# Gates and values of two chunks as seven products of halves, and a reordered start, in a pre-norm linear-attention block

## The chip, the cores and the metric

The kernel runs on one core of a Trainium2 chip. The metric is the device time of one execution in microseconds (us). Engines are named as in the profile: PE is TensorE (matrix products), PEld its weight loads, DVE is VectorE, ACT is ScalarE, POOL is GpSimd, SP is SyncE, which here issues nearly all DMAs. Each engine works through its own list of instructions in order; semaphores make one engine wait for another.

## What is computed

Input x is 4 sequences x 2048 tokens x 512 features, float32. Cut to what matters:

```python
xn  = layernorm(x)                                  # no gain
h   = layernorm(xn) * ln_g + ln_b                   # second normalisation, with gain
q, k, v = split(h @ W_qkv + b_qkv, 3)
gate = sigmoid(xn @ W_gate + b_gate); gate /= mean(gate) + EPS
q, k = relu(q * gate)**2 + EPS, relu(k * gate)**2 + EPS      # 16 heads of 32
# causal linear attention: running sums over time of k v^T and of k
out = (q . sum(k v^T)) / (q . sum(k) + EPS)
x = x + out @ W_proj + b_proj
y = layernorm(x)
x = x + gelu(y @ U1 @ V1 + b1) @ U2 @ V2 + b2       # rank 128, 2048 hidden
```

All products are float32. The profile counts one float32 product of a 128x128 block with 128x512 as two PE instructions.

## The kernel before, in words

The 8192 tokens are cut into 64 chunks of 128; a sequence has 16. Chunks are worked in pairs (c, c+1), c even. The order of the work is written out by hand (`tc.manual_schedule()`, line 748): the order of the calls is the order of the instructions on each engine.

- **Normalise.** `moments` (L213) takes mean and variance of a chunk on DVE. `first_norm_factors` (L321) makes scale and shift for four chunks at a time, for chunks from 4 on as a chain of small POOL instructions with Newton steps (`inverse_deviation_by_steps`, L227); `normalize_chunk` (L345) applies them on ACT. `turned` (L304) brings the chunk to features-first form through DRAM with SP's DMAs (`xlT`, four buffers).
- **Gates.** `gate_of` (L367): four products of a 128x128 block of `xlT` with 128x512 of the weights `wg` (L359), one DVE operation out of PSUM (L370), a sigmoid on ACT (L375), a factor on DVE (L379).
- **Queries and keys.** `combinations` (L383) forms four sums and differences of halves of the pair's `xlT` on POOL. `queries_and_keys` (L394) needs both results for both chunks, which is a 2x2 block product in halves (two chunks by two halves of the features; two halves by two outputs). It is done with seven half products instead of eight (the scheme of Strassen and Winograd); one half product is two matrix products. The weights lie in `w7` as seven slots (B11, B21, B22, T4, T1, T2, T3), the differences T1 to T4 are made once at the start (L786 to L789). `square` (L410) applies relu, gate and square, `turn_queries` (L468) and `turn_keys` (L473) turn the results in 32x32 blocks on DVE and through DRAM by DMA (L292 writes, L297 reads).
- **Values.** `values_of` (L460): four products with `wv` per chunk (L359), one DVE add (L463).
- **Attention of a chunk.** `new_keys` (L479) copies the last running sum into column 0 of `kT` on POOL; `keys_of` (L487) fills the rest on ACT; `sums_of` (L496) is a running sum on DVE (L500) and a product with the queries on POOL (L510); `scores_of` (L517) are 16 small products in four PSUM banks, masked by DVE (L534); `inverse_denominators` (L543) is a chain on DVE; `weighted` (L557) makes the numerator, multiplies by the inverse (L587) and adds k v to the state in PSUM (L596). `project_out` (L611) is the output projection, with the residual add (L617) and moments on DVE.
- **Feed-forward of a pair**, one pair behind: `feed_forward` (L649) is a list of small steps (`down`, 16 `hidden` L669 with gelu L671, 16 `gather` L675, two `up` L691). `pump(n)` (L704) emits the next n of them, and so fills PE's list between the steps of attention. `second_norm` (L623) prepares its input with Newton steps on POOL.
- **PSUM.** `bank` (L104) hands out six banks in turn; a product into a bank waits until the result that it held six requests ago was read.
- **The main loop** (L837) runs over pairs: combinations, gates, `down`, queries and keys, then scores and the rest of attention of the last chunk of the pair before (e = c - 1), then the first chunk of this pair, with the values' products between. `first_moments(n)` (L802) calls `first_norm_factors` at each fourth chunk.

Of the kernel before, what the change touches and what calls it, by code (L numbers as in the profile page):

```python
# [51 lines left out]
P = 128  # L53
# [4 lines left out]
def tile_linear_attention_block(  # L58
# [39 lines left out]
    xp = ctx.enter_context(tc.tile_pool(name="xp", bufs=13))  # L98
# [52 lines left out]
    wg, pieces = weights(w_gate, "wg")  # L151
    load(pieces)
    for c in range(1, NJ):
        load_x(c)
    wv, pieces = weights(w_qkv[:, 2 * D : 3 * D], "wv")
    load(pieces)
# [4 lines left out]
    w7 = const.tile([P, 7, NH, D], F32, tag="w7", name="w7")  # L161

    def load_half(slot, half, col):
        for k in range(NH):
            at = (half * NH + k) * P
            nc.sync.dma_start(w7[:, slot, k, :], w_qkv[at : at + P, col : col + D])

    load_half(B11, 0, 0)
    load_half(B21, 1, 0)
    bqkv_one = [row(b_qkv[bass.ts(n, D)], "a", 4, f"bqkv_one_{n}", nc.sync) for n in range(3)]  # L170
    load_half(B12, 0, D)
    load_half(B22, 1, D)
    load_x(NJ)
    wp, pieces = weights(w_proj, "wp")
    load(pieces)
    load_x(NJ + 1)
    load_x(NJ + 2)
# [10 lines left out]
    rows_of = [  # L188
        [w7[:, slot, k, :] for slot in (B11, B21) for k in range(NH)],
        [w7[:, slot, k, :] for slot in (B12, B22) for k in range(NH)],  # L190
        [wv[:, k, :] for k in range(NK)],
    ]
# [111 lines left out]
    def turned(src, to, name):  # L304
        st = blocks(src, name)
        dr = dram.tile([DH, NQ, NK, NQ, DH], F32, tag="drn", bufs=2, name=f"drn_{name}")
        for i in range(NQ):
            nc.sync.dma_start(
                dr[:, :, :, i, :].rearrange("m j k t -> m (j k) t"),
                st[i * DH : (i + 1) * DH].rearrange("m j k t -> m (j k) t"),  # L310
            )
        transfers_back()
        back.append(
            lambda: nc.sync.dma_start(
                to.rearrange("p k t -> p (k t)"), dr.rearrange("m j k i t -> j m (k i t)")
            )
        )
# [3 lines left out]
    def first_norm_factors(chunks, mv):  # L321
# [4 lines left out]
        if chunks[0] < NJ:  # L326
            inverse, engine = inverse_deviation, nc.vector
# [17 lines left out]
    def normalize_chunk(c):  # L345
        norm, n, _ = first_norm[c]
        xl = normalized(x_of[c], norm, n, f"xl_{c}")
        t = work.tile([P, NK, P], F32, tag="xlT", bufs=NJ, name=f"xlT_{c}")
        xlT_of[c] = t
        if c >= NJ:  # L350
            turned(xl, t, f"xl_{c}")

        return lambda: nc.scalar.copy(t, features_first(xl, f"ps_xl_{c}"))  # L353


    def project(c, w, name):
        ps = bank(name)
        for k in range(NK):
            nc.tensor.matmul(  # L359
                ps, xlT_of[c][:, k, :], w[:, k, :], start=(k == 0), stop=(k == NK - 1)  # L360
# [6 lines left out]
    def gate_of(c):  # L367
        ps = project(c, wg, f"ps_g_{c}")
        gate = work.tile([P, D], F32, tag="gate", bufs=2, name=f"gate_{c}")
        nc.vector.scalar_tensor_tensor(gate, ps, first_norm[c][2], bg_row, ALU.mult, ALU.add)  # L370
        return gate

# [21 lines left out]
    def queries_and_keys(c, s, gates):  # L394
# [4 lines left out]
        def half(ps, stationary, slot, more=False):  # L399
            for k in range(NH):  # L400
                nc.tensor.matmul(  # L401
                    ps,
                    stationary[:, k, :],
                    w7[:, slot, k, :],
                    start=(k == 0 and not more),
                    stop=(k == NH - 1),
                    skip_group_check=True,
                )

        def square(c, n, t):  # L410
            gate, rg = gates[c]
            nc.vector.scalar_tensor_tensor(t, t, 0.0, gate, ALU.max, ALU.mult)  # L412
            sq = work.tile([P, D], F32, tag="qk"[n], bufs=(2, 3)[n], name=f"{'qk'[n]}_{c}")
            nc.scalar.activation(sq, t, AF.Square, scale=rg)  # L414
            if n == 0:
                nc.scalar.activation(sq, sq, AF.Identity, bias=eps_col)
# [35 lines left out]
        def second():  # L452
            qT1 = turn_queries(c + 1, q1)
            kq1 = turn_keys(c + 1, k1)
            transfers_back()
            return {c: (k0, qT0, kq0), c + 1: (k1, qT1, kq1)}

        return second

    def values_of(c):  # L460
        ps = project(c, wv, f"ps_v_{c}")
        v = work.tile([P, D], F32, tag="v", bufs=2, name=f"v_{c}")
        return v, lambda: nc.vector.tensor_add(v, ps, bqkv_row[:, 2 * D : 3 * D])  # L463
# [79 lines left out]
    def inverse_denominators(c, qs):  # L543

        back = work.tile([P, H, DH], F32, tag="back", name=f"back_{c}")
        nc.vector.transpose(back.rearrange("p n d -> p (n d)"), qs.rearrange("p g t -> p (g t)"))
        den = work.tile([P, H], F32, tag="den", bufs=2, name=f"den_{c}")
        nc.vector.reduce_sum(den, back, axis=AX.X)
        nc.vector.tensor_scalar_add(den, den, EPS)
        nc.vector.reciprocal(den, den)  # L550
        inv = work.tile([P, NK, P], F32, tag="inv", name=f"inv_{c}")
# [97 lines left out]
    def feed_forward(b):  # L649
# [29 lines left out]
        def both(f):  # L679
# [4 lines left out]
            if f == NF + 1:  # L684
                held["qs"] = work.tile([P, BT], F32, tag="qs", name=f"qs_{b}")
# [29 lines left out]
    def spread(to, one, name):  # L715
        ps = bank(name)
        nc.tensor.matmul(ps, ones[0:1, :], one, start=True, stop=True)
        nc.scalar.copy(to, ps)
# [13 lines left out]
    def gain_in_weights(n):  # L732
        for k in range(NK):
            w = rows_of[n][k]
            nc.scalar.activation(w, w, AF.Copy, scale=g_col[:, k : k + 1])
# [15 lines left out]
    def gate_with_factor(c):  # L751
        gate = gate_of(c)
        total, rg = sigmoid_of(c, gate)
        return lambda: gate_factor(total, rg), (gate, rg)

    mv = new_moments("mv_0")
    gates, values = {}, {}
    moments(x_of[0], mv, 0)
    first_norm_factors([0], mv)
    spread(bg_row, bg_one, "ps_bg")  # L760
    spread(bp_row, bp_one, "ps_bp")
    normalize_chunk(0)()
    for c in range(1, NJ):
        moments(x_of[c], mv, c)
    first_norm_factors(range(1, NJ), mv)
    turn_xl = normalize_chunk(1)
    offset_terms(2)
    g0 = gate_of(0)
    turn_xl()
    gain_in_weights(2)  # L770
    offset_terms(0)
    g1 = gate_of(1)
    offset_sum(2)
    for c, g in ((0, g0), (1, g1)):
        total, rg = sigmoid_of(c, g)
        gate_factor(total, rg)
        gates[c] = g, rg
    gain_in_weights(0)
    offset_terms(1)
    gain_in_weights(1)  # L780
    for c in range(2):
        values[c] = values_of(c)
    turn_xl = [normalize_chunk(c) for c in (2, 3)]
    for c in range(2):
        values[c][1]()
    nc.vector.tensor_sub(w7[:, T1], w7[:, B12], w7[:, B11])  # L786
    nc.vector.tensor_sub(w7[:, T2], w7[:, B22], w7[:, T1])
    nc.gpsimd.tensor_sub(w7[:, T3], w7[:, B22], w7[:, B12])
    nc.gpsimd.tensor_sub(w7[:, T4], w7[:, B21], w7[:, T2])  # L789
    for turn in turn_xl:  # L790
        turn()
    offset_sum(0)
    offset_sum(1)
    spread(b2_row, b2_one, "ps_b2")


    mv_first = mv_second = None
    waiting = []
    pairs = {}
    keys = {}  # L800

# [10 lines left out]
    def sums_and_products(c, kT):  # L812
# [5 lines left out]

    def rest_of_attention(e, scores, inv):
        nonlocal mv_second  # L820
        oT = weighted(e, scores, pairs[e][1], pairs[e][0], values.pop(e)[0], inv)
        return oT
# [7 lines left out]
    finish = []  # L830

    def gates_in_step(c):
        for n in (c, c + 1):
            done, gates[n] = gate_with_factor(n)
            finish.append(done)

    for c in range(0, NC + 1, 2):  # L837
        e = c - 1
        live = c < NC

        if live:
            s_ = combinations(c)
            if c > 2:
                gates_in_step(c)
        if e > 0:
            nc.gpsimd.tensor_add(x_of[e], x_of[e], bp_row)
            inv = inverse_denominators(e, keys[e][1])

        if c >= 4:
            rest += feed_forward((c - 4) // NP)  # L850
            pump(1)
        if live:
            while finish:
                finish.pop(0)()
            if c > 0:
                first_moments(c + NJ + 2)
            second = queries_and_keys(c, s_, gates)
            gates.clear()
        else:
            waiting.pop(0)()  # L860
            transfers_back()
            pump(3)
        if e > 0:
            scores = scores_in_step(e)
        if live:
            pairs.update(second())
        pump(1)
        if live and c > 0:
            values[c] = values_of(c)
        pump(1)  # L870
        if e > 0:
            oT = rest_of_attention(e, scores, inv)
        if live and c > 0:
            values[c][1]()
        pump(1)
        if e > 0:
            project_in_step(e, oT)
            if live:
                kT = new_keys(c)
                waiting += second_norm([e - 1, e], mv_second)  # L880
# [10 lines left out]
        if c == 0:  # L891
            kT = new_keys(c)
            for n in range(NJ, NJ + 3):
                first_moments(n)
        if c + 7 < NC:
            load_x(c + 7)


        c, e = c + 1, c
        if c + 2 < NC:  # L900
            for n in (c + 1, c + 2):
                if n >= NJ:
                    normalize_chunk(n)
        sums_and_products(e, kT)
        nc.gpsimd.tensor_add(x_of[e], x_of[e], bp_row)
        kT = new_keys(c)
        if c == 1:
            gates_in_step(c + 1)
        pump(4)
        scores = scores_in_step(e)  # L910
        inv = inverse_denominators(e, keys[e][1])
        pump(3)
# [3 lines left out]
        if c > 1:  # L916
# [62 lines left out]
```

## Time and profile before

| | |
|---|---|
| runs (us) | 1914.93, 1919.36, 1915.3; median 1915.3 |
| profiled execution (us) | 1920.7 |
| its span (us) | 1918.9 |
| PE busy | 1867.0 us (97%) |
| DVE busy | 1197.8 us (62%) |
| POOL busy | 765.0 us (40%) |
| ACT busy | 646.1 us (34%) |
| mean granted PE clock | 0.988 |
| chain that ended last | PE 94%; DMA 2%; POOL, DVE, ACT, issue 1% each |
| gates (L359) of the pairs start at (us) | 130.16 (4, 5), 194.07 (6, 7), then every 56 to 58 us |

The span is the time from the first to the last instruction; the execution lasts 1.8 us longer. Busy time of PE is not PE at its peak, since the ends of its instructions overlap: 128x512 shows 0.59 us for one, but in a row one starts each 0.43 us. In the lines of a timeline the columns are start (us), duration (us), engine, line, operation, out<-in and count; brackets give the idle time ahead and what ended it.

### The profile page before, as it was taken

To read this page: it belongs to the slowest core of one execution; us is meant where nothing else is said; L and a number is where in the kernel's file an instruction comes from. 1 tells how busy PE (TensorE), PEld (TensorE's weight loads), DVE (VectorE), ACT (ScalarE), POOL (GpSimd) and SP (SyncE) were. 2 spreads that over 40 slices of the span, in tenths; PEclk is the share of its full clock that TensorE was granted. 3 is DMA by queue.
4 is the path that set the end of the run, shared out by engine and by line. 5 is a ranking of instruction groups with operands and counts; after the bars stand their busy time and mean duration, and the time that the engine had idled before them with its cause. 6 is when DMAs were issued, how large, how long until landed. Compare 5 with 4: busy or idle time off the path is not lost.

```text
span 1918.9 us, 34094 instructions
## 1 busy us (share of the span) xinstructions
PE 1867.0 (97%) x12832; PEld 1113.2 (58%) x12832; DVE 1197.8 (62%) x2107; ACT 646.1 (34%) x1112; POOL 765.0 (40%) x1578
## 2 busy tenths in 40 slices
PE   7679999999999999999999999999999999999988
PEld 3336555666555666555666655566655566655556
DVE  5566766566766666666666666666666666666651
ACT  4123333233333233333233333233333233333233
POOL 2433525353443533425353443534435343443330
PEclk9799999999999999999999999999999999999999
DMA  6133323333323333323333323333323333322220
GB/s 203 55 99 88 84 88 87 96 111 89 85 89 90 90 111 91 88 83 91 90 111 92 95 82 87 92 106 92 94 80 94 88 105 101 89 75 80 77 75 31
DMA packets 290577, 175.27 MB, mean 91 GB/s; under 512 B 138726, under 2 KB 239078, under 8 KB 290284
## 3 DMA queue, kind: packets, MB, share of 16 engines
q1 hardware_dynamic: 289350, 173.08, 30.7%
q8 instruction: 101, 1.65, 0.4%
q14 instruction: 64, 0.52, 0.1%
q10 hardware_dynamic: 1062, 0.01, 0.0%
HBM read 90.46 MB, written 82.58 MB: 90 GB/s over the span
## 4 chain that ended last, share of the span: by engine, by line
PE 94%; DMA 2%; POOL 1%; DVE 1%; ACT 1%; issue 1%; SPq 0%; ACTq 0%; DVEq 0%; POOLq 0%
PE ps_h L669 13%; PE ps_Q L675 12%; PE ps_q L401 11%; PE ps_p L614 11%; PE ps_v L359 11%; PE ps_g L359 11%; PE ps_a L524 4%; PE ps_n L578 3%; PE ps_n L567 3%; PE ps_u L401 3%; PE ps_t L401 3%; PE ps_P L656 3%; PE ps_k L401 3%; PE ps_u L691 3%; PE ps_S L596 1%
## 5 line engine op out<-in xcount | busy, mean ns | idle before, releaser
L671 ACT ACTIVATE h<-ps_h,b_col 128x256 f32<-128x256 f32 x512 | 242.5, 474 | 479.9 <-PE ps_h L669 479.6
L669 PE MATMUL ps_h<-pT,v_sb 128*128 128x256 f32 x1024 | 318.2, 393 | 9.2 <-DVE pT L664 9.2
L675 PE MATMUL ps_Q<-h,u_sb 128*128 128x256 f32 x1024 | 295.9, 381 | 1.0 <-ACT h L671 1.0
L614 PE MATMUL ps_p<-wp,oT 128*128 128x512 f32 x512 | 234.5, 601 | 6.3 <-DVE oT L587 6.3
L669 PEld LDWEIGHTS ps_h<-pT,v_sb 128*128 128x128 f32 x1024 | 185.0, 190 | 79.5 <-issue 37.1
L359 PE MATMUL ps_v<-wv,xlT 128*128 128x512 f32 x512 | 230.2, 592 | 0.0
L359 PE MATMUL ps_g<-wg,xlT 128*128 128x512 f32 x512 | 228.4, 599 | 1.4 <-ACT xlT L353 1.4
L675 PEld LDWEIGHTS ps_Q<-h,u_sb 128*128 128x128 f32 x1024 | 192.0, 190 | 31.9 <-ACT h L671 7.0
L401 PE MATMUL ps_q<-w,xlT 128*128 128x512 f32 x384 | 175.9, 594 | 0.0
L476 POOL TENSOR_SCALAR k<-k 128x512 f32<-128x512 f32 x64 | 95.8, 1498 | 199.8 <-DVE blocks_k L276 198.4
L534 DVE TENSOR_TENSOR a<-ps_a,causal 128x512 f32<-128x512 f32 x256 | 158.5, 680 | 25.1 <-PE ps_a L524 25.1
L617 DVE TENSOR_TENSOR x<-ps_p,x 128x512 f32<-128x512 f32 x64 | 44.3, 692 | 206.2 <-PE ps_p L614 163.1
L510 POOL TENSOR_TENSOR qsum<-qT,sums 128x512 f32<-128x512 f32 x64 | 75.3, 1176 | 241.7 <-DVE sums L500 234.0
L359 PEld LDWEIGHTS ps_g<-wg,xlT 128*128 128x128 f32 x512 | 98.2, 192 | 125.1 <-issue 118.5
L614 PEld LDWEIGHTS ps_p<-wp,oT 128*128 128x128 f32 x512 | 98.1, 193 | 104.6 <-issue 94.3
L375 ACT ACTIVATE gate<-gate 128x512 f32<-128x512 f32 x64 | 40.3, 629 | 335.7 <-DVE gate L370 335.7
L359 PEld LDWEIGHTS ps_v<-wv,xlT 128*128 128x128 f32 x512 | 97.1, 190 | 96.1 <-issue 92.6
L414 ACT ACTIVATE k<-u,rg 128x512 f32<-128x512 f32 x64 | 45.7, 714 | 308.6 <-DVE u L412 308.6
L233 POOL TENSOR_SCALAR newton_v<-mv 128x2 f32<-128x2 f32 (+2 forms) x48 | 11.7, 244 | 301.9 <-DVE mv L216 301.9
L401 PEld LDWEIGHTS ps_q<-w,xlT 128*128 128x128 f32 x384 | 73.3, 191 | 79.7 <-issue 69.9
L432 POOL TENSOR_TENSOR u<-u,t 128x512 f32<-128x512 f32 x32 | 40.5, 1265 | 197.0 <-DVE t L430 197.0
L370 DVE SCALAR_TENSOR_TENSOR gate<-ps_g,unscale,bg_row 128x512 f32<-128x512 f32 x64 | 47.9, 750 | 113.6 <-PE ps_g L359 113.6
(143 smaller groups left out, 2886.9 us busy)
## 6 DMA issues: line engine op xcount, KB each, us to landing
x<-in_L_attn_x_dram SPq DMA_DIRECT2D x64, 256.0 KB
dr_k<-blocks_k SPq DMA_DIRECT2D x64, 256.0 KB
dr_q<-blocks_q SPq DMA_DIRECT2D x64, 256.0 KB
kq<-dr_k SPq DMA_DIRECT2D x256, 64.0 KB
qT<-dr_q SPq DMA_DIRECT2D x256, 64.0 KB
out_dram<-x SPq DMA_DIRECT2D x64, 256.0 KB
dr_x<-blocks_x SPq DMA_DIRECT2D x63, 256.0 KB
x2T<-dr_x SPq DMA_DIRECT2D x252, 64.0 KB
```

The source lines that it names most:

```text
L359: nc.tensor.matmul(ps, xlT_of[c][:, k, :], w[:, k, :], start=(k == 0), stop=(k == NK - 1))
L401: nc.tensor.matmul(ps, stationary[:, k, :], w7[:, slot, k, :], start=(k == 0 and not more), stop=(k == NH - 1), skip_group_check=True,)
L476: nc.gpsimd.tensor_scalar_add(k, k, EPS)
L510: nc.gpsimd.tensor_mul(qs.rearrange("p k (i t) -> p k i t", t=DH), qT.rearrange("p i k t -> p k i t"), sums[:, :, 1 : P + 1].rearrange("p ...
L524: nc.tensor.matmul(ps[r][:, bass.ts(g, P)], kT[rows, g, 1 : P + 1], qT[rows, :, g, :], start=True, stop=True,)
L534: nc.vector.tensor_tensor(a, ps[r].rearrange("p (g t) -> p g t", t=P), causal.unsqueeze(1).to_broadcast([P, NK, P]), ALU.mult,)
L567: nc.tensor.matmul(num[rows, bass.ts(g, P)], S[rows, g, :], qT[rows, :, g, :], start=(g == 0), stop=False, skip_group_check=True,)
L578: nc.tensor.matmul(num[r * DH : (r + 1) * DH, bass.ts(g, P)], v[:, h * DH : (h + 1) * DH], scores[r][:, g, :], start=first and g == 0, sto ...
L614: nc.tensor.matmul(ps, oT[:, g, :], wp[:, g, :], start=(g == 0), stop=(g == NK - 1))
L669: nc.tensor.matmul(ps, v1_sb[:, 0, bass.ts(f, P)], held["p"], start=True, stop=True)
L671: nc.scalar.activation(h, ps, AF.Gelu_apprx_tanh, bias=b1_col[:, f : f + 1])
L675: nc.tensor.matmul(held["q"], u2_sb[:, f, :], held["h"].pop(f), start=(f == 0), stop=(f == NF - 1))
```

## The change

Three parts, made together:

1. **Gates and values of a pair** (c >= 4) become one 2x2 block product of halves, with seven half products instead of eight: `gates_and_values`. It uses the pair's `combinations`, which queries and keys have already, and a second set of seven weight slots, `wgv` (gate weights in B11 and B21, value weights in B12 and B22); `w7` is now `wqk`, and `wg` and `wv` are gone. To make room, `xlT` has two buffers instead of four, x tiles 12 instead of 13, the queries are squared in place, and some tiles share buffers.
2. **The start** is written out anew for the first two pairs: gates and values of these are still plain products; pair (2, 3) gets its projections before the attention of chunks 0 and 1. Factors of chunks 4 to 7 are made on ACT and DVE.
3. **The loop** runs for pairs from 4 on, in a new order: inverse denominators of e, x loads, gates and values, scores of e, queries and keys, `down`, the rest of attention of e, and so on. `new_keys` moves into `sums_and_products`; the first moments of two chunks stand together, ahead of it.

```diff
-    xp = ctx.enter_context(tc.tile_pool(name="xp", bufs=13))
+    xp = ctx.enter_context(tc.tile_pool(name="xp", bufs=12))
...
-        if chunks[0] < NJ:
+        if chunks[0] < 2 * NJ:
             inverse, engine = inverse_deviation, nc.vector
...
-        t = work.tile([P, NK, P], F32, tag="xlT", bufs=NJ, name=f"xlT_{c}")
-        xlT_of[c] = t
+        def new_tile():
+            if c not in xlT_of:
+                xlT_of[c] = work.tile([P, NK, P], F32, tag="xlT", bufs=2, name=f"xlT_{c}")
+            return xlT_of[c]
...
+    def gates_and_values(c, s):
+
+        a, b = xlT_of[c], xlT_of[c + 1]
+        lo, hi = slice(0, NH), slice(NH, NK)
+        ps1 = bank(f"ps_g_{c}")
+        half_product(ps1, a[:, lo], wgv, B11)
+        t1 = temp(f"g1_{c}")
+        nc.scalar.copy(t1, ps1)
+        ps2 = bank(f"ps_gu_{c}")
+        half_product(ps2, s[:, 1], wgv, T2)
+        u2 = temp(f"gu2_{c}")
+        nc.vector.tensor_add(u2, ps2, t1)
+        ps5 = bank(f"ps_g_{c + 1}")
+        half_product(ps5, s[:, 2], wgv, T3)
+        u3 = temp(f"gu3_{c}")
+        nc.vector.tensor_add(u3, ps5, u2)
+        half_product(ps1, a[:, hi], wgv, B21, more=True)
+        g0 = new_gate(c)
+        gate_input(c, g0, ps1)
+        done = [sigmoid_of(c, g0)]
+        half_product(ps5, b[:, hi], wgv, T4, more=True)
+        g1 = new_gate(c + 1)
+        nc.vector.tensor_add(g1, ps5, u2)
+        gate_input(c + 1, g1, g1)
+        done.append(sigmoid_of(c + 1, g1))
+        ps3 = bank(f"ps_gt_{c}")
+        half_product(ps3, s[:, 0], wgv, T1)
+        t5 = temp(f"g5_{c}")
+        nc.vector.tensor_add(t5, ps3, bqkv_row[:, 2 * D : 3 * D])
+        v0 = new_values(c)
+        nc.gpsimd.tensor_add(v0, u2, t5)
+        ps4 = bank(f"ps_v_{c}")
+        half_product(ps4, s[:, 3], wgv, B22)
+        v1 = new_values(c + 1)
+        nc.gpsimd.tensor_add(v1, u3, t5)
+        nc.vector.tensor_add(v0, ps4, v0)
...
-    def sums_and_products(c, kT):
+    def sums_and_products(c):
+        kT = new_keys(c)
         keys_of(kT, pairs[c][2])
         keys[c] = kT, sums_of(c, kT, pairs[c][1])
...
+    second = queries_and_keys(0, combos.pop(0))
+    combine(2)
+
+    second()
+    transfers_back()
+    g2 = gate_of(2)
+    for n in range(NJ, 2 * NJ):
+        first_moments(n)
+    g3 = gate_of(3)
+    sums_and_products(0)
+    sigmoids((2, 3), (g2, g3))
+    values_of(2)
+    scores = scores_in_step(0)
+    inv = denominators_in_step(0)
+    for n in (8, 9):
+        load_x(n)
+    second = queries_and_keys(2, combos.pop(2))
+    transfers_back()
+    sums_and_products(1)
+    oT = rest_of_attention(0, scores, inv)
+    scores = scores_in_step(1)
...
+    for c in range(NJ, NC + 1, 2):
+
         e = c - 1
         live = c < NC
+        inv = denominators_in_step(e)
         if live:
+            for n in (c + 6, c + 7):
+                if n < NC:
+                    load_x(n)
+            gates_and_values(c, combos[c])
+            if c == NJ:
+                project_in_step(2, oT)
...
+        scores = scores_in_step(e)
+        if live:
+            second = queries_and_keys(c, combos.pop(c))
+
+        rest += feed_forward((c - 4) // NP)
+        pump(1)
...
+        oT = rest_of_attention(e, scores, inv)
         if live:
+            transfers_back()
+            second()
+            for n in (c + 6, c + 7):
+                first_moments(n)
+        pump(4)
+        project_in_step(e, oT)
...
+        transfers_back()
+        sums_and_products(c)
+        waiting += second_norm([e - 1, e], mv_second)
         pump(4)
+        scores = scores_in_step(c)
+        inv = denominators_in_step(c)
+        pump(4)
         while waiting:
             waiting.pop(0)()
         transfers_back()
+        oT = rest_of_attention(c, scores, inv)
+        if c + 2 < NC:
+            combine(c + 2)
+        pump(6)
+        project_in_step(c, oT)
...
         pump(len(rest))
+        sums_and_products(c + 1)
+        normalize_pair(c + 4)
```

## The prediction, made before the changed kernel was run

> **What bounds the kernel now.** I first read the page's busy shares and slices, then a table of busy time by stretches, then PE's timeline at the start. The slices:
>
> ```profile
> PE   7679999999999999999999999999999999999988
> PEclk9799999999999999999999999999999999999999
> ```
>
> After the third slice PE is full and its clock is granted. One stretch of 57 us in the table by windows (columns: busy time and instructions of PE, PEld, DVE, ACT, POOL, then clock, DMA share, GB/s):
>
> ```profile
> 257.00:314.00 57.00, 57.00 (x408) 34.37 (x407) 37.03 (x65) 19.60 (x33) 25.70 (x65) 1.00 0.32 93
> ```
>
> From 160 to 1860 us PE shows no idle time; DVE and POOL are under two thirds and under half. A PE instruction less is a gain there, unless PE starts to wait. The idle time is some 37 us ahead of 160 us, and 15 us at the end (8.65 of it for DVE's pT), which both kernels share. At the start PE waits for transfers and combinations:
>
> ```profile
> 31.16 1.36 PE L266 MATMUL ps_xl<-ident,xl 128*128 128x128 f32 x8 [2.06 <-ACT xl L257]
> 39.06 3.03 PE L401 MATMUL ps_u<-w,combos 128*128 128x512 f32 x4 [1.86 <-POOL combos L389]
> 64.87 2.09 PE L524 MATMUL ps_a<-qT,kT 32*128 32x128 f32 x32 [6.67 <-DMA qT<-dr_q]
> 87.79 3.59 PE L401 MATMUL ps_u<-w,combos 128*128 128x512 f32 x4 [7.27 <-POOL combos L389]
> ```
>
> **A. Products saved.** One half product is four instructions (two products):
>
> ```profile
> 490.26 1.88 PE L401 MATMUL ps_q<-w,xlT 128*128 128x512 f32 x4
> 491.98 1.88 PE L401 MATMUL ps_u<-w,combos 128*128 128x512 f32 x4
> ```
>
> Their starts lie 1.72 us apart, 0.43 each. Gates and values of a pair fall from eight half products to seven: 1.72 saved. That holds for 30 pairs, 51.6 in all; I count the 29 from pair (6, 7) on here, **-49.9**, and the first in the start. The period of a pair is 57.5 before (56.25 at a sequence's ends), and would be 55.8 if nothing waited.
>
> **B. A wait in the gates, each pair.** In the new loop the inverse denominators of e stand ahead of the gates on DVE, and so do the running sums, the residual add, moments, both `up` adds of the last feed-forward and two blocks_xl transposes. From the start of the gate products the DVE list, by its own rows, is: 1.45 ahead, residual add and moments (0.7, 0.7, 0.2); `up` adds to 1.3 (0.67 each); scan to 2.4 (1.21); two transposes to 3.7 (0.68 each). POOL's qsum (1.18) runs beside these from 2.55 to 3.7. Then come the five rows of the denominators, 0.7, 0.7, 0.2 to 0.3, 0.25 and 0.7, to 6.4, and only then gu2 and gu3 (0.7 each) to 7.8:
>
> ```profile
> 545.65 0.70 DVE L546 STREAM_TRANSPOSE back<-qsum 128x512 f32<-128x512 f32 x1
> 546.38 0.69 DVE L548 TENSOR_REDUCE den<-back 128x16 f32<-128x512 f32 x1
> 547.10 0.33 DVE L549 TENSOR_SCALAR den<-den 128x16 f32<-128x16 f32 x1
> 547.47 0.25 DVE L550 RECIPROCAL den<-den 128x16 f32<-128x16 f32 x1
> 547.75 0.71 DVE L552 STREAM_TRANSPOSE inv<-den 128x512 f32<-128x512 f32 x1
> ```
>
> The fifth half product (T4) adds into the bank that gu3 must have read. It is due on PE after four others, 4 x 1.72 = 6.9, and starts at 7.9. Price 1.0 a pair. Queued behind it on PE are the last two half products and all of the pair. Bounds: 0.3 (the small row takes 0.3 and not 0.7, transposes packed) and 1.3 (it takes 0.7 to 1.1, as one row at 524.27 shows). x29 = **+29** (9 to 38).
>
> **C. A wait for Newton steps, every second pair.** The first moments of two chunks now stand ahead of `new_keys`. At every second pair they bring the chain of `first_norm_factors`, and on POOL the copy into column 0 of kT stands behind all of it. The chain before, first and last row, and what follows:
>
> ```profile
> 531.41 0.23 POOL L233 TENSOR_SCALAR newton_v<-mv 128x4 f32<-128x4 f32 x1 [4.82 <-DVE mv L216]
> ...
> 539.34 1.05 POOL L242 TENSOR_SCALAR newton_t<-newton_t 128x4 f32<-128x4 f32 x1
> ...
> 541.95 0.20 POOL L339 TENSOR_TENSOR unscale<-unscale,scale 128x4 f32<-128x4 f32 x1
> 542.13 1.18 POOL L510 TENSOR_TENSOR qsum<-qT,sums 128x512 f32<-128x512 f32 x1
> ```
>
> 35 instructions, 10.7 us; one took 1.05, beside a DVE scan. Before, the scan at 539.19 ran in the middle of the chain, since its copy stood ahead of it. Now the scan cannot: it needs the copy. Behind the scan on DVE stand the four masks of scores(c), and PE's score banks, of six in turn, are wanted again by the feed-forward. Count from the end t of the query and key products. PE: `down` 1.7, numerator and state 2.4, six feed-forward products 2.6 (0.43 each), projection 3.4, eight more products 3.5: scores start at 13.8, end near 14.9; two feed-forward products run, and the third at 16.7 needs a bank that a mask must have read. DVE: pT, oT (0.69, behind the numerator), the copy of S, two block transposes and two moments end at 7.7. POOL: chain of 9.9 (10.7 less the 0.85 that the one slow row lost) to 17.6, copy 0.2; DVE: scan 1.1, mask 0.7: 19.7. PE waits **3.0**. After that qsum ends at 20.3, the 16 instructions of the second norm (4.4) at 24.7, two normalisations on ACT at 26.2; a gelu is queued behind these, 0.47 more, and PE wants its result at 26.2: about 0.7. Together 3.7; bounds 2.0 (moments 1 us earlier, the second wait hidden) and 5.5 (more slow rows in the chain). It happens for c = 8, 12, ..., 56: 13 x 3.7 = **+48** (26 to 72). In the pairs between the copy stands behind two eps adds only, no wait.
>
> **D. xlT with two buffers.** SP's read into xlT now waits for the last product of the old one, t - 1.7, and SP's later issues (x, dr_k, dr_q) stand behind it. Writes land in some 4.1 us and reads in 4 to 5 by the rows before, so kT and qT are there at t + 11 to 13.6, against scores at 13.8. I take 0.3 (0 to 1.0) for the 16 ordinary pairs: **+5**.
>
> **Other edits, at nothing.** Square in place and shared tiles: ACT (31%) and DVE (62%) hide them. The new adds (g1, g5, v0, v1: four on DVE and two on POOL of 0.7, less two value adds) fit in: DVE 37 of 57 us becomes some 39. If that cover went, each would cost at most its 0.7.
>
> **E. The start.** Chunks 2 and 3 get gates and values while chunk 0 goes through DRAM (51.20 to 64.87 before): 10.3 us of products cover most of those 13.7, and the wait falls from 6.7 to 3.3. The weight differences on POOL start earlier, so the first query and key block ends at 43.5 instead of 51.2. Queries and keys of pair (2, 3) follow and end near 71 (99.9 before, with the 7.27 us for combinations). Lost again: some 4 us where kT of chunk 1 stands behind a square on ACT, some 7 and 4 us in the first new gate block near 97 (ACT's copy behind normalisations that wait for POOL's chain; DVE's gu3 behind denominators), 3 for half clock after these. Queries and keys of pair 4 end at 140 instead of 157; with 34 us more, from there to the next gates, the gates of pair (6, 7) start at 177 instead of 194.07: **-17** (-30 to -5), the product saved in pair (4, 5) in it.
>
> **Sum.** -49.9 + 29 + 48 + 5 - 17 = +15. The profiled execution is 1920.7 (span 1918.9 and 1.8 around it): 1935.7. The runs' median, 1915.3, lies 5.4 lower, so **1930**.
>
> **The clock.** After a wait the granted clock can fall: in the table of windows it is 0.50 from 40 to 42 us, after the 1.86 us gap at 39.06, and eight instructions took 5.2 instead of 3.4 there, 1.8 lost. After 2.06 (31.16) and 1.81 us (113.04) it did not fall; after each gap of 4.5 and more it did. By these rows the 3.0 of C costs 0 to 1.8 each; I take nothing, since two of the three near gaps cost nothing, and 13 x 1.8 = 23 as the upper end. [...]
>
> **Rivals.**
> 1. *The other side: the copy comes in time.* If the chain's end and the copy lie 3 us earlier against PE (DVE's moments before the block transposes' waits, PE slower than I place it), C is gone: 1930 - 48 = **1882**. It turns to faster by 0.3% once the wait is 2.1 or less instead of 3.7 (1.6 x 13 = 21, 1909). For it: C is a difference of two long sums, 19.7 against 16.7. Against: the chain's 9.9 is measured, and nothing on POOL can pass it.
> 2. *The clock falls after each Newton wait*: +23, **1953**. For it the row at 39.06, against it the two others.
> 3. *PE stays full*: no B, C, D: 1930 - 29 - 48 - 5 = **1848**. For it: before, PE never waited in the loop, at similar shares of DVE. Against: the T4 product's bank and the order of POOL's list.
> 4. *Between*: the start gains 10 us more or C is 1 us less: within 0.3%, 1910 to 1921.
>
> **Numbers.** 0.3%, 6 us, is about what a measurement of this kernel can tell from no change. Forecast 0.42; rival 2 0.13; rival 4 0.13; rival 1 0.22; rival 3 0.10. Slower 0.42 + 0.13 = 0.55, same 0.13, faster 0.32. The unknown costs alone (B -20 to +9, C -22 to +24, E -13 to +12, D 5) give some 1895 to 1956 around 1930. The range, 1880 to 1956, takes in rivals 1, 2 and 4 and leaves out rival 3 and half of what lies beyond 1's edge. The forecast's own range is 1921 to 1945.
>
> **What would show it.** In the profile after: PE's `hidden` waiting about 3 us for DVE's mask, 13 or 14 times; DVE's scan waiting for POOL's copy into kT at these places; the T4 product waiting about 1.0 for gu3 in each pair; gates of pair (6, 7) at 177; ordinary periods near 57.0, those with a chain near 60.6; clock 1.00 in the loop. It is wrong if PE shows no idle time in the loop (then 1848), if the gates of pair (6, 7) start after 194, or if the wait at the masks is under 2.

## The result, and the profile after

The changed kernel takes 1996.1 us (median of 4 runs, 1993.5 to 1999.4) against 1917.1 (4 runs): ratio 1.0413, interval 1.0391 to 1.0435. It is 4.1% slower. The forecast was 1930, slower by 0.8%, with 1956 as the upper end of its range: the sign was right, the size not. The profiled execution has a span of 1991.7 us, 72.8 longer than before; the sum of the prediction was +15.

The slices of the page after:

```profile
PE   8889999999899999999989999999999999999988
PEclk9989999999999999999999999999999999999999
```

The first three slices are fuller than before (the new start), and two later ones are down to 8: PE now waits in the loop. It was busy for 1593 of the 1700 us between 160 and 1860, where it had been busy for all. What PE waited for over the whole span (us in total, times, longest):

```profile
PE ps_Q L739 <- ACT h L735: 53.9, 45, 2.5
PE ps_g L411 <- DVE gu L435: 26.6, 30, 1.5
PE ps_a L588 <- DMA qT<-dr_q: 24.1, 28, 2.6
PE ps_h L733 <- DVE a L598: 10.7, 14, 0.9
```

The second row is part B of the prediction, the fourth the mask wait of part C. The first and third were not forecast at this size. They belong together, as runs 1 and 2 below show. In one ordinary pair (one without a Newton chain of the first norm) PE's timeline shows them with B's:

```profile
548.01 1.98 PE L411 MATMUL ps_g<-wgv,xlT 128*128 128x512 f32 x4 [0.86 <-DVE gu L435]
...
580.75 0.70 PE L739 MATMUL ps_Q<-h,u_sb 128*128 128x256 f32 x2 [1.43 <-ACT h L735]
...
583.01 1.17 PE L588 MATMUL ps_a<-qT,kT 32*128 32x128 f32 x32 [0.70 <-DMA qT<-dr_q]
```

The gelu that the second one waits for stands on ACT behind kT, and kT behind a transfer:

```profile
579.61 0.72 ACT L553 ACTIVATE kT<-kq,eps_col 128x512 f32<-128x512 f32 x1 [5.75 <-DMA kq<-dr_k]
```

So both are waits for keys and queries of the pair's first chunk on their way through DRAM. SP's queue in the same pair (columns: start and duration of the issue; t, the end of the query and key products, is 566.58):

```profile
565.10 0.55 SPq L317 DMA_DIRECT2D xlT<-drn_xl  x1
565.70 1.48 SPq L113 DMA_DIRECT2D x<-in_L_attn_x_dram  x2
567.22 0.43 SPq L294 DMA_DIRECT2D dr_k<-blocks_k  x1
568.17 0.56 SPq L317 DMA_DIRECT2D xlT<-drn_xl  x1
568.94 0.41 SPq L294 DMA_DIRECT2D dr_q<-blocks_q  x1
572.75 2.18 SPq L299 DMA_DIRECT2D kq<-dr_k  x4
576.08 2.38 SPq L299 DMA_DIRECT2D qT<-dr_q  x4
```

The first xlT read is held until PE is done with the old xlT, t - 1.5; the two x loads stand behind it, and dr_k, whose blocks were ready at 564.97, behind these. Before, in a pair with t = 502.28, xlT and x moved elsewhere:

```profile
500.63 0.33 SPq L292 DMA_DIRECT2D dr_k<-blocks_k  x1
504.61 0.32 SPq L292 DMA_DIRECT2D dr_q<-blocks_q  x1
505.04 2.21 SPq L297 DMA_DIRECT2D kq<-dr_k  x4
508.69 2.31 SPq L297 DMA_DIRECT2D qT<-dr_q  x4
```

From t, dr_k is 2.3 us later than before in this pair (1.7 to 1.8 in most ordinary pairs), the read of kq 3.4 and that of qT 3.1.

Periods from `down` to `down`: 13 ordinary pairs 59.9 us in the mean (forecast 57.0), the 13 with a chain 61.6 (forecast 60.6), against 57.5. The two ordinary pairs that come after the last x loads last only 57.8 and 58.1. The start came as forecast: the gates of pair (6, 7) begin at 176.2 (forecast 177, before 194.07). Its new waits:

```profile
60.59 1.17 PE L588 MATMUL ps_a<-qT,kT 32*128 32x128 f32 x32 [2.61 <-DMA qT<-dr_q]
...
112.17 3.78 PE L411 MATMUL ps_g<-wgv,xlT 128*128 128x512 f32 x4 [6.98 <-ACT g L427]
117.45 3.71 PE L411 MATMUL ps_g<-wgv,xlT 128*128 128x512 f32 x4 [1.50 <-DVE gu L435]
```

The first was forecast as 3.3, the others as some 7 and 4. From the last `down` to the end it is 22.9 us in both kernels.

### The profile page after: what moved, and what is told of

The parts are those of the page before. It is cut to its first block, busy times and chain, and to the rows that moved or that the text cites. A ratio compares the mean times of both kernels' runs of the same rounds, so it can differ in the third digit from the quotient of the medians.

```text
span 1991.7 us, 34034 instructions
## 1 busy us (share of the span) xinstructions
PE 1843.2 (93%) x12712; PEld 1081.3 (54%) x12712; DVE 1248.1 (63%) x2210; ACT 650.1 (33%) x1142; POOL 806.3 (40%) x1607
## 4 chain that ended last, share of the span: by engine, by line
PE 49%; DVE 17%; DMA 17%; POOL 8%; issue 5%; SPq 2%; ACT 2%; DVEq 0%; ACTq 0%; POOLq 0%
PE ps_q L411 8%; PE ps_Q L739 7%; PE ps_h L733 6%; DMA dr_k<-blocks_k 5%; PE ps_p L678 5%; DMA dr_q<-blocks_q 5%; DMA qT<-dr_q 4%; PE ps_g L411 3%; PE ps_u L411 3%; PE ps_a L588 3%; PE ps_t L411 3%; DVE sums L564 3%; PE ps_gt L411 3%; PE ps_v L411 3%; PE ps_k L411 2%
## 5 line engine op out<-in xcount | busy, mean ns | idle before, releaser
L733 PE MATMUL ps_h<-pT,v_sb 128*128 128x256 f32 x1024 | 307.5, 392 | 20.9 <-DVE a L598 10.7
L735 ACT ACTIVATE h<-ps_h,b_col 128x256 f32<-128x256 f32 x512 | 225.8, 471 | 233.8 <-PE ps_h L733 233.4
L411 PE MATMUL ps_g<-wgv,xlT 128*128 128x512 f32 x360 | 176.0, 612 | 33.6 <-DVE gu L435 26.6
L411 PE MATMUL ps_q<-wqk,xlT 128*128 128x512 f32 x372 | 172.9, 600 | 0.0
L564 DVE TENSOR_TENSOR_SCAN sums<-keep,kT 128x516 f32<-128x516 f32 x64 | 78.6, 1228 | 127.1 <-POOL kT L548 81.5
L411 PEld LDWEIGHTS ps_g<-wgv,xlT 128*128 128x128 f32 x360 | 66.8, 193 | 131.9 <-issue 71.9
L450 POOL TENSOR_TENSOR v<-gu,g 128x512 f32<-128x512 f32 x30 | 38.0, 1265 | 224.3 <-DVE g L448 224.3
L411 PEld LDWEIGHTS ps_q<-wqk,xlT 128*128 128x128 f32 x372 | 68.2, 190 | 78.2 <-issue 74.4
L553 ACT ACTIVATE kT<-kq,eps_col 128x512 f32<-128x512 f32 x64 | 45.9, 717 | 197.3 <-DMA kq<-dr_k 197.1
L588 PE MATMUL ps_a<-qT,kT 32*128 32x128 f32 x2048 | 75.5, 283 | 27.6 <-DMA qT<-dr_q 24.1
```

The lines of the kernel that those rows point to most:

```text
L411: nc.tensor.matmul(ps, stationary[:, k, :], w[:, slot, k, :], start=(k == 0 and not more), stop=(k == NH - 1), skip_group_check=True,)
L553: nc.scalar.activation(kT[:, :, 1 : P + 1].rearrange("p k (i t) -> p k i t", t=DH), kq.rearrange("p i k t -> p k i t"), AF.Identity, bias= ...
L564: nc.vector.tensor_tensor_scan(sums.rearrange(flat), keep.rearrange(flat), kT.rearrange(flat), 0.0, ALU.mult, ALU.add,)
L588: nc.tensor.matmul(ps[r][:, bass.ts(g, P)], kT[rows, g, 1 : P + 1], qT[rows, :, g, :], start=True, stop=True,)
L733: nc.tensor.matmul(ps, v1_sb[:, 0, bass.ts(f, P)], held["p"], start=True, stop=True)
L735: nc.scalar.activation(h, ps, AF.Gelu_apprx_tanh, bias=b1_col[:, f : f + 1])
```

## The experiments

All start from the changed kernel. "Theory" is the one that its expectation names.

**1. Is it ACT's order?** The sums of chunk c are emitted behind four feed-forward steps:

```diff
-        sums_and_products(c)
         waiting += second_norm([e - 1, e], mv_second)
         pump(4)
+        sums_and_products(c)
```

> The changed kernel with one move: the column copy, ACT's kT, the scan and qsum of chunk c are emitted behind the four feed-forward steps that follow the projection, instead of ahead of them, so no gelu of these steps stands behind kT on ACT. Changed kernel: profiled time 1993.5, period 59.6 us in ordinary pairs, 61.5 in those with a chain; per pair PE waits 1.5 for a gelu there and then 0.7 to 0.9 for qT. Theory 1 (keys and queries land late; the two waits are one): the wait for the gelu goes, the wait for qT or kT ahead of the scores grows by the same 1.5, time within 8 us of 1993. Theory 2 (ACT's order is what costs): the gelu wait goes and nothing takes its place, -1.5 x 29 = -44, about 1950.

Measured: 2090.5 (one run). The gelu wait went, and the wait for qT took its place and more; the mask wait grew too, since the scan now starts later:

```profile
PE ps_a L588 <- DMA qT<-dr_q: 76.9, 30, 3.8
PE ps_h L733 <- DVE a L598: 47.6, 17, 3.6
```

Theory 2 falls: the transfer is what is late, not ACT's order. But theory 1 expected no change, and the time rose by 94. The clock is most of the answer: its mean is 0.955, against 0.991 in the changed kernel. The table by windows (the clock is the third column from the end) shows it behind the gaps of 2.43 us at 606.77 and 3.78 at 669.34:

```profile
607.00:611.00 4.00, 4.00 (x39) 3.30 (x36) 3.79 (x6) 0.47 (x1) 2.59 (x4) 0.57 0.16 47
...
670.00:674.00 4.00, 4.00 (x34) 3.32 (x31) 0.00 (x0) 0.47 (x1) 2.89 (x15) 0.50 0.19 55
```

Behind one wait of 2.4 us or more, in place of two short ones, the clock stood at a half, for some 160 us in the loop in all (7 us in the changed kernel). Half of the difference, some 77 us, is an estimate of what that cost of the 94. The ordinary pairs show it best: the one of 13 whose clock stayed full lasts 59.65, as in the changed kernel and as theory 1 says; the other 12 last 61.1 to 62.0. The rest of the 94 stands in the pairs with a chain, where the mask wait grew.

**2. The transfers out of the way.** The xlT reads of the next pair go behind the reads of the second chunk; the x loads thereby leave at the loop's head. xlT keeps two buffers.

```diff
-        back.append(
+        (late if held else back).append(
             lambda: nc.sync.dma_start(
                 new_tile()...
...
         transfers_back()
+        while late:
+            late.pop(0)()
         sums_and_products(c)
...
+        held.append(1)
         normalize_pair(c + 4)
+        held.clear()
```

> The changed kernel with SP's order altered: the two xlT reads of the next pair are issued behind the reads of this pair's second chunk, not ahead of dr_k, so that x loads go out at the loop's head and dr_k, dr_q, kq, qT of the first chunk have the queue and the engines for themselves. xlT still has two buffers. Theory 1 (the late transfers cost PE some 2.7 us a pair): ordinary pairs 59.6 -> 57.0; in pairs with a chain the wait at the masks, 0.65 in the changed kernel, grows towards the 3.0 forecast, 61.5 -> 60.5. Together 16 x -2.6 + 13 x -1.0 = -55, about 1939. If the order of the new loop costs by itself (gates, ACT's list), no more than -10.

Measured: 1945.3, ratio to before 1.0149 (1.0130 to 1.0168): 51 less than the changed kernel. SP's queue in a pair with t = 555.7:

```profile
554.12 0.33 SPq L296 DMA_DIRECT2D dr_k<-blocks_k  x1
558.06 0.33 SPq L296 DMA_DIRECT2D dr_q<-blocks_q  x1
558.50 2.24 SPq L301 DMA_DIRECT2D kq<-dr_k  x4
560.91 2.45 SPq L301 DMA_DIRECT2D qT<-dr_q  x4
```

From t these are where they were before (kq) or earlier (qT). Ordinary pairs last 57.09, as theory 1 expected, and of the two waits little is left over the whole span:

```profile
PE ps_Q L741 <- ACT h L737: 5.8, 11, 1.4
PE ps_a L590 <- DMA qT<-dr_q: 3.2, 2, 2.3
```

In the pairs with a chain, 60.9 in the mean, C now has about its forecast size:

```profile
514.81 0.70 PE L735 MATMUL ps_h<-pT,v_sb 128*128 128x256 f32 x2 [2.23 <-DVE a L600]
521.80 0.70 PE L741 MATMUL ps_Q<-h,u_sb 128*128 128x256 f32 x2 [1.34 <-ACT h L737]
```

The mask wait, 0.65 in the changed kernel, is 2.2 to 2.5: PE no longer arrives late for it. In 8 of these 13 pairs the clock fell to a half behind this wait, and PE took 1.5 to 1.7 us longer for the same products there. Away from a sequence's ends a pair lasts 60.5 where it stayed full and 61.5 where it fell.

**3. B taken away.** `inv = denominators_in_step(e)` is emitted behind `gates_and_values` instead of ahead of it.

> The changed kernel with the inverse denominators of e emitted behind the gates and values instead of ahead of them. Theory (B of the prediction): gu2 and gu3 come some 2.6 us earlier on DVE, the 0.87 wait of the T4 product goes, 30 x -1.0 = -30, about 1963. Rival: the 2.6 us of DVE work now delay the masks and the first adds of queries and keys, and PE waits for a bank there: 0 to -10.

Measured: 1961.4 (one run), 35 less. The wait for gu3 is gone from the loop, and the periods fall by 1.1, as expected. But the run doesn't price B alone. A new wait of 0.44 for a gelu stands in each pair, and some 0.7 is lost in the query and key block. The wait for the late keys takes these up: in an ordinary pair its gelu part falls from some 1.5 to some 0.5. Run 5 shows what is left of this move when the keys aren't late.

**4. C's copy taken away.**

```diff
+            kT = new_keys(c)
             for n in (c + 6, c + 7):
                 first_moments(n)
```

> The changed kernel with only the copy into column 0 of kT (new_keys) moved back ahead of the two first moments, so that it stands ahead of the Newton chain on POOL. Theory (C as measured: the mask wait is the copy's): the wait for the masks (0.65 to 0.9 at 14 places, 10.7 in all) goes, and the wait for a gelu behind the second norm (1.35) stays, since qsum still stands behind the chain: 13 x -0.9 = -12, about 1982. If C had its forecast size, 13 x -3.7 = -48, about 1945.

Measured: 1984.7 (one run), 11 less. The mask wait is gone, the gelu wait stays (54.9 us in all). With the transfers still late, the copy is worth little.

**5. The three moves together.**

> The changed kernel with the three moves together: xlT reads behind the reads of the second chunk, the column copy ahead of the first moments, the inverse denominators behind the gates. If the three waits are separate, ordinary pairs go from 57.1 (reads moved alone) to 56.1; pairs with a chain from 60.2-61.5 to about 57.6, if the 1.35 us wait for a gelu behind the second norm stays, and 56.1 if it goes too. From 1945: -30 for the gates and 13 x -2.2 to -4.5: 1860 to 1890, point 1880, faster than the kernel before by some 35. If one wait hides behind another again, 1895 to 1920.

Measured: 1932.5, ratio to before 1.0086 (1.0072 to 1.0100): only 13 less than the reads alone. The expectation missed. Ordinary pairs last 57.22, not 56.1, though no product waits for gu3. In one of them the distances from one PE start to the next show 0.8 us lost in the query and key block: three groups there (ps_q, ps_t, ps_q) start late by 0.10, 0.33 and 0.37, where a step is 0.43, with no idle time shown in the timeline (0.10 in run 2). A wait of 0.44 for a gelu also stands in each pair. Together they use up B's 1.1. And dr_k left at t - 0.9 instead of t - 1.6. The denominators behind the gates stand ahead of DVE's masks and adds: the first add of queries and keys starts at t - 7.4, in run 2 at t - 9.3. Pairs with a chain still wait:

```profile
515.67 0.70 PE L741 MATMUL ps_Q<-h,u_sb 128*128 128x256 f32 x2 [2.66 <-ACT h L737]
```

**6. The same with plain products.** Gates and values as in the start, four half products each. Here the upper half of the values' weights is read from the slot that by then holds T3; the work is that of plain products.

```diff
-            gates_and_values(c, combos[c])
+            sigmoids((c, c + 1), (gate_of(c), gate_of(c + 1)))
+            for n in (c, c + 1):
+                values_of(n)
```

> The same three moves, but gates and values of all pairs as four plain half products each (16 matrix products instead of 14, wgv's plain slots): 4 x 0.43 = 1.72 more PE work in each of 30 pairs. If the seven products are worth their full term A once nothing waits: 51.6 slower than the three moves with seven products. If their adds on DVE, POOL and ACT cost part of it: 20 to 45. Here no product waits for gu3, so that term B cannot occur.

Measured: 1955.4, 22.9 more. Ordinary pairs 58.01 against 57.22: of the 1.72 saved, 0.8 arrived there.

**7. Queue or sharing?** Only the x loads are moved, ahead of the xlT writes at the end of the pair before.

> The changed kernel with only the two x loads moved: they are issued ahead of the xlT writes at the end of the pair before, so that between the held xlT read and dr_k nothing stands on SP. The xlT reads stay beside dr_k and dr_q. Queue theory (dr_k is late because two issues of 1.5 us stand ahead): dr_k goes out 1.5 earlier, ordinary pairs 59.6 -> 58.2, about 1993 - 16 x 1.4 - 13 x 0.8 = 1960. Sharing theory (dr_k and dr_q land 1 to 2.5 us later since the xlT reads and x loads move bytes at the same time): with the x bytes out of the way but the xlT bytes still there, half of the 2.6 or more goes: 1945 to 1965. Neither (the held read itself): 1985 to 1993.

Measured: 1960.1 (one run), 36 less; ordinary pairs 58.2. From t, in the median of the 13 ordinary pairs, dr_k leaves at -0.9, kq's read at +4.8, qT's at +8.1 (changed kernel: +0.1, +6.4, +9.8; reads moved: -1.6, +2.8, +5.2). So the two x loads ahead on SP are 1.6 to 1.7 of the delay of the reads, and 1.7 of the period. The changed kernel agrees: its two ordinary pairs without x loads last 57.8 and 58.1. The rest, 2.0 for kq and 2.9 for qT, and 1.1 of the period, comes with the xlT reads, which are still there: in ordinary pairs dr_k to its read takes 5.3 to 5.8 us beside them, 4.4 without (run 2). Whether that is bytes shared or an order among the transfers isn't told apart.

**8. Denominators earlier, not later.** Sums and denominators of c + 1 are emitted at the end of the pair:

```diff
         oT = rest_of_attention(c, scores, inv)
+        sums_and_products(c + 1, kT)
         if c + 2 < NC:
             combine(c + 2)
         pump(6)
+        inv_next = denominators_in_step(c + 1)
         project_in_step(c, oT)
```

> The changed kernel with the xlT reads and the column copy moved as in the three moves, but the inverse denominators not behind the gates: the scan, qsum and the inverse denominators of chunk c + 1 are emitted at the end of the pair, ahead of its last projection, where DVE sat idle for some 6 us in the changed kernel. Theory: DVE's list between the start of the gates and the end of queries and keys is full, so that what is put behind the gates only moves the wait (three moves: no wait for gu3, but starts in the query and key block 0.8 us late and dr_k 0.7 us late); put ahead, the 1.0 is saved for good. Ordinary pairs 57.1 -> 56.1; pairs with a chain, where the second norm still stands behind the chain on POOL, 58 to 60; about 1903. If placing does not matter: as the three moves, 1925 to 1935.

Measured: 1929.2, ratio to before 1.0063 (1.0043 to 1.0082). Ordinary pairs came down to some 56.5, as expected. Pairs with a chain did not (59.4 to 62.2): with POOL's qsum and second norm behind the chain as before, one wait stands there, and where the clock falls behind it (9 of 13 pairs), the pair is 1.4 to 2.8 longer than the 59.35 of those where it doesn't:

```profile
517.14 1.22 PE L741 MATMUL ps_Q<-h,u_sb 128*128 128x256 f32 x2 [3.83 <-ACT h L737]
```

**9. The chain put off too.** `first_moments` keeps the chain back; it is emitted at the end of the pair, and `normalize_pair(c + 2)` behind the gates.

```diff
+            factors.append(lambda: first_norm_factors(chunks, mv))
...
         pump(len(rest))
+        while factors:
+            factors.pop()()
```

> As the run before, and the Newton chain of the first norm moved to the end of the pair on POOL, behind combinations and qsum, where POOL sat idle for some 15 us; the normalisation of the next pair stands behind its gates. No copy, qsum or second norm stands behind the chain any more. Theory: C is a matter of POOL's order alone, so that all pairs become ordinary, 56.1 to 56.6 us. From 1945: 29 x -1.0 for the gates and 13 x -3.8 for the chain: about 1867 (1850 to 1890), faster than the kernel before by 1.4 to 3.4%. If the pairs with a chain stay dearer by 2 or more, the chain is not what they wait for.

Measured: 1872.5, ratio to before 0.9764 (0.9750 to 0.9779): 2.4% faster than the kernel before, 124 less than the changed one. All pairs last 55.9 to 57.2; the clock was full from 160 us to the wait at the end (1820). What PE waited for:

```profile
PE ps_Q L741 <- ACT h L737: 13.4, 22, 2.0
PE ps_g L413 <- ACT g L429: 6.6, 1, 6.6
```

**10. The same with plain products**, as in 6.

> The kernel of the run before (chain put off, 1872.5) with gates and values of the pairs from (4, 5) on as four plain half products each, 16 matrix products instead of 14. The upper half of the values' weights is read from the slot that by then holds T3, so the values are other numbers, the work is that of the plain products. With PE full in both, the seven products are worth their term A: 30 x 4 x 0.43 = 51.6 more, 1924 (1915 to 1930). In the three moves, where PE waited, they were worth 22.9. If their adds still cost PE something here, 20 to 40.

Measured: 1906.2, 33.8 more than run 9; the expectation was too high. The period of a pair in which PE shows no wait is 57.67 against 55.96: 1.71, A as forecast. But in the mean over the loop it is 57.9 against 56.4, since with seven products PE has more small waits, for a gelu above all (29 x 1.46 = 42), and the start is 8 us earlier without them (`down` of the first pair at 135.5 against 143.8), because the waits of 6.6 and 1.5 in the first new gate block do not occur.

## Why the prediction was wrong, step by step

- **A holds.** 1.71 a pair by the pairs of runs 9 and 10 that show no wait. The full 51.6 arrives nowhere, since small waits come with it and the first gate block adds 8 us.
- **B holds**: 0.87 us of idle time in each pair. The two half products on either side of it take 4.55 us from start to start (545.28 to 549.83 in the changed kernel) in place of 2 x 1.72, 1.1 more, and the periods say the same (57.09 in run 2's ordinary pairs, 55.96 in those of run 9 that show no wait); forecast 1.0.
- **C holds in mechanism, but not in the changed kernel, and its size is partly luck.** Alone (run 2) a pair with a chain is 3.8 longer than an ordinary one, forecast 3.7. But that is 3.4 where the clock stayed full and 4.4 where it fell, and the mask wait is 2.2 to 2.5 and not 3.0, the gelu wait up to 1.3 and not 0.7. In the changed kernel such a pair is only 1.7 longer, and the mask wait of 0.5 to 0.9 is under the 2 that the prediction itself names as a sign of being wrong: there PE is already late by D when it reaches the masks.
- **D is the step that failed**, "I take 0.3 (0 to 1.0) for the 16 ordinary pairs: +5". Its mechanism, the held xlT read with dr_k behind it, was named; its size was wrong nearly tenfold. On top of the forecast periods it cost 2.9 in 13 ordinary pairs, 0.8 and 1.1 in the two without x loads, and 1.0 in the 13 others: 53 of the 58 by which the sum missed the span. Some 4 more are the three pairs at a sequence's end, 56.25 before, which are no shorter than the others now. (The median of the runs misses by 66, as it lies 2.6 above the profiled execution and not 5.4 below.) That it is D is shown by run 2, where the reads alone are moved and ordinary pairs come to 57.1, forecast 57.0. Two things went into the size: the issues ahead of dr_k delayed it by 1.7 to 2.3, and the durations of write and read were taken from a trace in which neither xlT nor x moved beside them: from dr_k's issue to the read of qT the DMA engines were 0.24 busy in the pair of before shown above (500.6 to 508.7), and 0.56 in the changed kernel's (567.2 to 576.0). I had kT and qT at t + 11 to 13.6, and scores due at 13.8; kT began at t + 13.0 and qT came at t + 16.4. I also did not say that kT on ACT has gelus queued behind it, so that PE waits 1.5 before the scores are even due (run 1: part of the same wait, not another).
- **E holds**, partly by luck: -17.9, forecast -17. The waits inside came at 2.6, 7.0 and 1.5 against 3.3, some 7 and 4, and the first query and key block ended at 47.5, not 43.5. The prediction's 140 and 34 also make 174 and not its 177; measured are 141.2 and 35.1.
- **Other edits, at nothing**: the two new POOL adds take 1.27 us each and not 0.7, but PE shows no wait for them.
- **Rivals.** That the copy comes in time (1) did not happen; its reason was half right, since PE was slower than placed, but what held PE cost more. PE did not stay full (3). The fall of the clock (2) played almost no part in the changed kernel, but in runs 1, 2 and 8 it did, behind gaps of 2.2 us and more.

No one length of a gap decides in these runs whether the clock falls. In run 2, 8 of 13 gaps of 2.2 to 2.5 us were followed by half clock, in run 1 18 of 19 gaps of 2.3 to 2.65; in the changed kernel's loop none of the 11 between 1.5 and 1.9 was, and two of the four between 2.0 and 2.6. But in run 8, 4 of 13 gaps of 3.1 to 3.8 us left the clock full, and in run 5 all three of 2.65 to 2.66 did, while 3 of 9 of 1.9 to 2.0 did not. The changed kernel's loop has two stretches at half clock, 824.1 to 827.5 and 1189.3 to 1192.7; both lasted 3.4 us.

Open is which part of the xlT reads' harm is bytes and which is order; more xlT buffers, which the change gave up to make room for the second set of weights, were not tried.

## What to carry to other kernels

Price a transfer that is held for a buffer by what stands behind it in its queue and by the round trip that now runs beside it, not by the durations of a trace in which its bytes move elsewhere, and ask what stands behind the landing on each engine. Here dr_k, behind the held xlT read and the x loads, left 1.7 to 2.3 us later than before, and from dr_k to its read it took 5.3 to 5.8 us beside the xlT reads (run 7) and 4.4 without (run 2). Don't add up the waits of one pair: the three moves together (run 5) were expected 65 us below the reads alone (run 2), and came 13 below. Here each wait hid the next, as the mask wait, 0.65 us in the changed kernel, grew to 2.2 to 2.5 in run 2, so a fix was worth its size only once the wait ahead of it was gone. The order of the fixes decided what each seemed to be worth: the denominators and the copy took 35 and 11 us alone (runs 3 and 4), and 13 together behind the reads. A saved product arrived in full, 1.71 us a pair, only in pairs where PE had no other wait (runs 9 and 10); where it had some, 0.8 arrived (runs 5 and 6). Undoing what the new order cost on SP's, POOL's and DVE's lists was worth more here (124 us) than the products (34). Against the kernel before, the mended order with plain products (run 10) gains 10 us, and the seven products make it 44.

## What was not expected of the hardware

Two short gaps cost less here than one long one in their place: two waits of 1.43 and 0.70 us (changed kernel, at 580.75 and 583.01) left the clock at 1.00; behind one of 2.43 (run 1, at 606.77) it was 0.57 in the mean over the next 4 us, and it fell to a half in 12 of run 1's 13 ordinary pairs. PE's steps also got longer with no idle time shown: 0.8 us in run 5's query and key block, visible only in the distance from start to start.
